# Two query tiles to a unit in a sparse attention, and conditioning by pairs of weight units

## The chip, the core and the metric

The kernel runs on one core of a Trainium2 chip: one program, one launch. The metric is the device time in microseconds (us), measured from outside the program; the profile's span is the time from the first to the last instruction on the core. The core has a matrix engine, TensorE (PE in the profile, PEld for its weight loads, PEq for its instruction queue), and VectorE (DVE), ScalarE (ACT), GpSimd (POOL) and SyncE (SP), which here issues most of the DMAs. The engines run side by side and wait for each other through semaphores. Each works through its own instructions in the order in which the program was written.

## What is computed

Four layers in a row on x (4 batches, 512 tokens, 512 channels), each steered by a vector of 512 numbers per batch. All numbers are float32.

```python
x = L0(x, cond)   # adaptive layer norm, sparse attention: 16 heads of 32, 4 key/value heads
x = L1(x, cond)   # adaptive RMS norm, attention: 8 heads of 64 on one key head; gated MLP of 2048
x = L2(x, cond)   # adaptive layer norm, attention: 16 heads of 32 with a bias; MLP of 2048
x = L3(x, cond)   # 8 experts of 64 channels, norm scaled and shifted by cond, output projection
```

The part that matters is layer 0:

```python
h = layernorm(x) * (1 + scale) + shift            # scale, shift: products of cond with W_ada
q = rope(h @ Wq.T); c = h @ Wkd.T
k, v = rope(c @ Wku.T), c @ Wvu.T                 # 4 heads, each used by 4 query heads
mask = (abs(i - j) > 64) & (j % 64 != 0) | (j // 128 > i // 128)    # hidden keys
y = softmax(q @ k.T / sqrt(32), hidden keys left out) @ v
x = x + y @ Wo.T
```

A tile of 128 queries therefore sees at most 197 keys: those of its own block of 128 and of the 64 before it (192 in all, or 128 for the first tile), and the earlier ones at multiples of 64 (1, 3 or 5).

The conditioning makes, from the vectors of the 4 batches, products with ten square weight matrices of 512 (tw1 and tw2 for layer 1; six for layer 2: two scales, two shifts, two gates; two for layer 3). In all but the first two, silu is taken of the vector first.

## The kernel before

**An order that is planned.** The kernel first runs as a plan. Every engine call and every matmul is recorded together with a start time that a small table of costs gives it (class Clocks); at the end all calls are sorted by these starts and emitted. So each engine's order is fixed when the program is built, and the chip's semaphores see to it that nothing starts too early.

**Streams.** Two streams of stages are woven together (interleave, streams A and M): layer 0 and layer 1's attention of a batch (a01), layer 1's MLP (m1), layer 2's attention (a2), layer 2's MLP with layer 3 (m2). A stage is a generator; it yields the amount of work just planned, or the time until which it must wait (Until), and the loop goes on with the stream that lags. At first batch 0 runs its a01 on stream M and batch 1 its own on stream A, both without an MLP beside them. From then on one stream has an attention while the other has an MLP. The conditioning is a third generator that moves when a stage asks for its result (wanted) or when no stream is ready.

**Units of attention.** The function attention takes units one by one: it issues the scores of unit i + 1, then turns the softened probabilities of unit i with TensorE's transposes (back), and, once two units have been turned, multiplies both with the values. The scores need all four PSUM banks of the pool psS (two_banks, a ring of 2); transposes and values use single banks (side.bank).

In layer 0 a unit is a pair (c, qt): four heads (one chunk c of 128 channels) and one tile of 128 queries, 16 units for each batch. Its steps are:

- scores: four matmuls with 32 rows each, in the four quarters of the array's rows, side by side; they write 128 to 197 columns into four banks.
- softmax: DVE adds the mask, scales and takes the lowest (lowest); ACT exponentiates and sums (soften); DVE takes the reciprocal of two sums; POOL multiplies. All of it runs in two halves of two heads.
- back: four transposes of the first 128 keys into a bank, and a copy into pT (evict, on ACT or DVE, whichever the plan has free); then four of the other 65 to 69 keys, if there are any, and another copy.
- values: for two units at once, matmuls with 32 columns each in the four quarters of the array's columns.

A run of matmuls on TensorE that follow each other in the same form of the array is called a run below. The forms here are the whole array (128*128 in the profile: projections, MLPs, transposes), row quarters (32*128: scores), column quarters (128*32: values and the conditioning's products with the vectors), and halves of both kinds (64*128 and 128*64).

**Conditioning.** For each of its ten weight units, partial makes four products with the vectors, one for each chunk of 128 rows, in the four column quarters; the result is evicted to rows. A second stage sums the four quarters: the matrix four has ones where a partition belongs to a batch, and four small matmuls (one per chunk) give the sums with channels on partitions. For the two gates one matmul of 512 columns gives them with batches on partitions, and they go to DRAM. The weight units pass one by one through a single buffer (ringC, tag late); the next is loaded when the products with the one before have been planned. Layer 1's norm asks for n1, its MLP for n2, layer 2 for all.

All engine calls of DVE, ACT, POOL and SP go through one wrapper and carry line 325 in the profile (load: line 391); matmuls have line 378, transposes line 384. So the profile's groups are told apart by their tiles: two are score banks, bank other PSUM banks, probs and wm the probabilities of the two streams, pT and hid the turned ones, arow the rows of the conditioning.

Of the kernel before, what the change touches and what calls it, by code (L numbers as in the profile page):

```python
# [19 lines left out]
P = 128  # L20
# [312 lines left out]
def cond_seq_kernel(ctx: ExitStack, tc: tile.TileContext, a: dict, out: bass.AP):  # L333
# [232 lines left out]
    cT, sT = (const.tile([P, NC, 32], F32, name=s) for s in ("cT", "sT"))  # L566
    gpsimd.memset(cT, 0.0)
    gpsimd.memset(sT, 0.0)
    four = const.tile([P, B], F32, name="four")
    vector.tensor_reduce(four, ident.rearrange("p (j b) -> p b j", b=32)[:, 0:B, :], axis=AX.X, op=ALU.add)  # L570
# [18 lines left out]
    vector.tensor_copy(cT[:, :, 0:B], condv)  # L589
    scalar.activation(sT[:, :, 0:B], condv, AF.Silu)  # L590
# [204 lines left out]
    def attention(side, units, scores, back, values, work, first, final=True):  # L795
# [21 lines left out]
        for i, u in enumerate(units):  # L817
            cost, more = 0.0, i + 1 < len(units)
            when = [scorable] if more else []
            if len(late) == 2:  # L820
                yield Until(*when, side.at, of=late[0][1] + late[1][1])
                values(late)
                late = []
                cost += 2 * work[1]
            else:
                yield Until(0.0, *when)
# [111 lines left out]
    def attention0(b, side):  # L938
# [71 lines left out]
        def scores(u):  # L1010
            c, qt = u
            first, near, seen = keys_of(qt)
            n = near + seen
            s = [two_banks() for _ in range(2)]
            for g in range(4):
                mm(
                    s[g // 2][:, g % 2, 0:n], lhsT=qT[quarter(g), c, qt * P : (qt + 1) * P],
                    rhs=kT[quarter(g), qt, 0:n], start=True, stop=True,
                )
            bias = mask[:, WIN - near : WIN + seen] if seen else mask[:, 64:WIN]  # L1020
            p = side.probs(WIN + 8)
            for q, sc in zip(p, s):
                soften(q, q, lowest(q, sc, bias, n, 1.0 / math.sqrt(32.0)), n, -1.0)
            return p, lambda: None
# [5 lines left out]
        def back(u, p, then):  # L1030
            if then:
                then()
            pT = part_of(side.pT(1)[0], 0, (2, 512))
            for i, (at, n) in enumerate(blocks(u[1])):
                yield Until(side.at, of=[q[:, :, at : at + n] for q in p])
                ps = side.bank()
                for g in range(4):
                    tr(ps[0:n, g * P : (g + 1) * P], p[g // 2][:, g % 2, at : at + n], ident)
                evict(pT[0:n, i, :], ps[0:n, :])
                yield 0.45  # L1040
            return [pT]

        def values(two):
            o, (c, first) = side.bank(), two[0][0]
            for k, ((_, qt), (pT,)) in enumerate(two):
                bl = blocks(qt)
                for i, (at, n) in enumerate(bl):
                    for g in range(4):
                        mm(
                            o[quarter(g), k * P : (k + 1) * P], lhsT=v[0:n, qt, i, quarter(g)],  # L1050
                            rhs=pT[0:n, i, g * P : (g + 1) * P], start=i == 0, stop=i == len(bl) - 1,
                        )
            evict(ctxT[:, c, first * P : (first + 2) * P], o[:, 0 : 2 * P])

        units = [(c, qt) for c in range(NC) for qt in range(NT)]
        yield from attention(side, units, scores, back, values, (0.7, 0.7), [qT, kT], False)
# [413 lines left out]
    def conditioning(side):  # L1470
        def partial(unit, cond):

            ps = side.bank()
            for i in range(NC):
                mm(
                    ps[32 * i : 32 * i + 32, :], lhsT=cond[:, i, :], rhs=unit[:, i, :], start=True, stop=True
                )
            rows = buf("arow", 2, (P, 512))
            evict(rows, ps)
# [4 lines left out]
        def product(name, cond):  # L1484

            unit = ringC.take(name)
            yield Until(side.at, of=[unit, sT])
# [306 lines left out]
```

## Time and profile before

| | us |
|---|---|
| three runs | 2446.61, 2450.02, 2448.89 |
| median | 2448.89 |
| the profiled execution | 2445.96 |
| its span | 2444.2 |
| TensorE's mean granted clock in it | 0.994 of full speed |

Groups of the profile that touch layer 0's units and the conditioning, all four batches (mean of one, number):

| group | mean ns | number |
|---|---|---|
| DVE: mask and lowest, 193 to 197 columns (probs) | 355 to 360 | 144 |
| DVE: mask and lowest, 128 columns (probs) | 287 | 48 |
| ACT: exponential, 193 to 197 columns (probs) | 446 to 450 | 144 |
| ACT: its sum read out (all exponentials on probs from SBUF) | 187 | 448 |
| DVE: reciprocal of two sums (all layers) | 165 | 320 |
| POOL: product with the reciprocal, 193 to 197 columns (probs) | 429 to 440 | 144 |
| ACT: copy of turned probabilities, 512 columns | 577 | 231 |
| DVE: the same | 683 | 172 |
| ACT: table load | 1283 | 32 |
| TensorE: bank<-four,arow, 4 columns (records) | 250 | 80 |

Durations of TensorE's records overlap, because matmuls are pipelined; what one costs is read from the starts of the ones that follow each other. A float32 matmul of the program leaves two records, a transpose one.

### The profile page before, as it was taken

Reading aid. Unit: us, or ns where it says so; the run is one execution under the profiler, and the core shown is the slowest. Engines: PE = TensorE matmul, PEld = TensorE weight load, DVE = VectorE, ACT = ScalarE, POOL = GpSimd, SP = SyncE. Lnnn points to the kernel's source line nnn. Section 1 sums busy time; section 2 is a strip of 40 time slices with the busy share of each in tenths; the row PEclk is TensorE's granted clock in tenths of the full one; section 3 lists DMA queues with packets and bytes.
Section 4 is the critical chain, followed back from the end, with each engine's and each line's share of the span. In section 5 each row is a group of like instructions: output and inputs, shape, how many; then the busy total and the mean of one; then the engine's idle time right before and its main releaser. Section 6 shows DMA issues by size and latency. Waiting matters only on the chain.

```text
span 2444.2 us, 33286 instructions
## 1 busy us (share of the span) xinstructions
PE 2408.0 (99%) x12586; PEld 1259.4 (52%) x12586; DVE 1118.8 (46%) x2886; ACT 870.0 (36%) x2088; POOL 725.8 (30%) x920
## 2 busy tenths in 40 slices
PE   8999999999999999999999999999999999999998
PEld 5555654444554555554455455564455544554444
DVE  5656452233654344535454445454455333673233
ACT  3745441002551351414454044241355202561213
POOL 5633320003332223323332222433322203442321
PEclk9999999999999999999999999999999999999999
DMA  3220212220112111121220212112211122112210
GB/s 112 70 74 34 72 69 70 90 87 35 35 53 92 54 67 56 36 73 46 80 70 29 97 53 74 52 40 73 73 48 53 61 80 88 36 36 88 89 52 26
DMA packets 80239, 154.17 MB, mean 63 GB/s; under 512 B 3584, under 2 KB 6688, under 8 KB 80080
## 3 DMA queue, kind: packets, MB, share of 16 engines
q1 hardware_dynamic: 79472, 151.83, 18.0%
q8 instruction: 100, 1.64, 0.3%
q14 instruction: 59, 0.48, 0.1%
q0 software_dynamic: 176, 0.15, 0.1%
q10 hardware_dynamic: 432, 0.07, 0.0%
HBM read 147.83 MB, written 4.21 MB: 62 GB/s over the span
## 4 chain that ended last, share of the span: by engine, by line
PE 95%; DVE 2%; ACT 1%; POOL 1%; DMA 1%; issue 1%; POOLq 0%; ACTq 0%; DVEq 0%
PE bank L378 72%; PE bank L384 12%; PE two L378 11%; ACT probs L325 1%; PE two L384 0%; DMA wm<-in_units 0%; DVE mn L325 0%; DVE mx L325 0%; ACT wm L325 0%; POOL inv L325 0%; DMA x<-in_x 0%; DVE nq L325 0%; POOL probs L325 0%; POOL rstd L325 0%; DMA arow<-in_rows 0%
## 5 line engine op out<-in xcount | busy, mean ns | idle before, releaser
L325 POOL TENSOR_SCALAR probs<-probs,inv 128x512 f32<-128x512 f32 (+4 forms) x544 | 316.3, 596 | 681.9 <-DVE inv L325 630.6
L325 ACT ACTIVATE probs<-probs,neg 128x512 f32<-128x512 f32 (+2 forms) x448 | 265.5, 594 | 215.6 <-DVE neg L325 209.6
L384 PEld LDWEIGHTS bank<-ident,probs 128*128 128x128 f32 (+2 forms) x1744 | 205.3, 141 | 162.8 <-issue 136.0
L378 PE MATMUL bank<-mT,wm_gate 128*128 128x512 f32 x512 | 246.9, 595 | 0.0
L384 PE MATMUL bank<-ident,probs 128*128 128x128 f32 (+2 forms) x1744 | 245.1, 275 | 0.8 <-POOL probs L325 0.4
L378 PE MATMUL bank<-mT,wm_up 128*128 128x512 f32 x512 | 245.5, 597 | 0.0
L378 PE MATMUL bank<-wm_down,hid 128*128 128x512 f32 x496 | 231.7, 596 | 0.0
L325 DVE CUSTOM_DVE_ANT_0 probs<-two,late 128x512 f32<-128x512 f32 x256 | 166.4, 688 | 79.2 <-PE two L378 48.1
L378 PE MATMUL bank<-wm_fc,hid 128*128 128x512 f32 x384 | 187.7, 593 | 0.0
L378 PE MATMUL bank<-mT,wm_fc 128*128 128x512 f32 x384 | 182.2, 596 | 0.0
L325 ACT COPY pT<-bank 128x512 f32<-128x512 f32 (+2 forms) x263 | 147.1, 577 | 82.7 <-PE bank L384 74.7
L325 ACT ACTIVATE mt<-bank 128x512 f32<-128x512 f32 x64 | 37.9, 591 | 322.2 <-PE bank L378 322.2
L378 PE MATMUL two<-kT,nq 32*128 32x512 f32 (+5 forms) x1088 | 149.8, 538 | 0.8 <-ACT probs L325 0.8
L325 DVE TENSOR_TENSOR x<-x,bank 128x512 f32<-128x512 f32 x98 | 66.9, 682 | 169.4 <-PE bank L378 169.4
L378 PEld LDWEIGHTS bank<-mT,wm_up 128*128 128x128 f32 x512 | 90.7, 190 | 97.8 <-issue 97.0
L378 PEld LDWEIGHTS bank<-mT,wm_gate 128*128 128x128 f32 x512 | 91.1, 190 | 94.7 <-issue 94.7
L378 PEld LDWEIGHTS bank<-wm_down,hid 128*128 128x128 f32 x496 | 89.2, 190 | 95.9 <-issue 94.2
L378 PEld LDWEIGHTS bank<-pT,v 128*32 128x32 f32 (+2 forms) x3488 | 112.7, 116 | 47.9 <-issue 28.1
L378 PE MATMUL bank<-pT,v 128*32 128x128 f32 (+2 forms) x3488 | 130.5, 274 | 0.0
L325 DVE COPY pT<-bank 128x512 f32<-128x512 f32 (+2 forms) x176 | 118.4, 683 | 22.3 <-PE bank L384 21.7
L325 POOL TENSOR_TENSOR rstd<-var,neg_half 128x4 f32<-128x4 f32 (+1 forms) x25 | 24.7, 991 | 347.5 <-DVE var L325 340.2
L378 PE MATMUL bank<-wa_q,h 128*128 128x512 f32 x272 | 127.7, 595 | 0.0
(283 smaller groups left out, 3363.7 us busy)
## 6 DMA issues: line engine op xcount, KB each, us to landing
wm_fc<-in_units SPq DMA_DIRECT2D x24, 1024.0 KB, 5.1
wm_gate<-in_units SPq DMA_DIRECT2D x16, 1024.0 KB, 5.1
wm_up<-in_units SPq DMA_DIRECT2D x16, 1024.0 KB, 5.5
wm_down<-in_units SPq DMA_DIRECT2D x16, 1024.0 KB, 5.4
wa_q<-in_units SPq DMA_DIRECT2D x10, 1024.0 KB, 5.0
wa_fc<-in_units SPq DMA_DIRECT2D x8, 1024.0 KB, 5.1
wa_o<-in_units SPq DMA_DIRECT2D x6, 1024.0 KB, 5.8
wa_k<-in_units SPq DMA_DIRECT2D x4, 1024.0 KB
```

Source lines behind the costliest of these rows:

```text
L325: return call(*map(real, args), **{k: real(x) for k, x in kw.items()})
L378: latest[0] = nc.tensor.matmul(real(out), lhsT=real(lhsT), rhs=real(rhs), **kw)
L384: latest[0] = nc.tensor.transpose(real(out), real(src), unit)
```

## The change

**Layer 0.** A unit becomes (c, (qt, qt + 1)): four heads and two query tiles, 8 units for each batch. Eight score matmuls fill both halves of each of the four banks, 256 columns apart. The softmax works on four parts at a time (two heads, two tiles) in each of its two halves; there is one reciprocal of four sums. The second half is planned in the midst of the transposes of the unit before, as in the other layers' attention. Transposes go by half and key block: both tiles' first blocks share a bank and one copy of 512 columns; the second blocks share a bank and are copied tile by tile (256 columns). Values follow each unit (group=1).

**Conditioning.** The vectors lie at columns 4 to 7 of 36 in cT and sT. A slice of 32 columns that begins at 4 puts them on rows 0 to 3 of each quarter, one that begins at 0 on rows 4 to 7. So two weight units' products are added (together) and one second stage with eight columns serves both. The ten units go in five pairs; the two gates are stored by one DMA.

```diff
-    cT, sT = (const.tile([P, NC, 32], F32, name=s) for s in ("cT", "sT"))
+    cT, sT = (const.tile([P, NC, 36], F32, name=s) for s in ("cT", "sT"))
-    four = const.tile([P, B], F32, name="four")
+    four = const.tile([P, 2 * B], F32, name="four")
...
-    def attention(side, units, scores, back, values, work, first, final=True):
+    def attention(side, units, scores, back, values, work, first, final=True, group=2):
...
-            if len(late) == 2:
-                yield Until(*when, side.at, of=late[0][1] + late[1][1])
+            if len(late) == group:
+                yield Until(*when, side.at, of=sum((pT for _, pT in late), []))
                 values(late)
                 late = []
-                cost += 2 * work[1]
+                cost += group * work[1]
...
         def scores(u):
-            c, qt = u
+            c, qts = u
             s = [two_banks() for _ in range(2)]
+            for k, qt in enumerate(qts):
+                first, near, seen = keys_of(qt)
+                for g in range(4):
+                    mm(
+                        s[g // 2][:, g % 2, 256 * k : 256 * k + near + seen],
+                        lhsT=qT[quarter(g), c, qt * P : (qt + 1) * P], rhs=kT[quarter(g), qt, 0 : near + seen],
+                        start=True, stop=True,
+                    )
+            p = side.probs(512)
+            def soft(i):
+                neg, total, inv = (tiny([P, 4], x) for x in ("neg", "total", "inv"))
...
+                for x, (q, sc, bias) in enumerate(parts):
+                    vector.tensor_tensor_reduce(
+                        out=q, in0=sc, in1=bias, scale=-1.0 / math.sqrt(32.0), scalar=HIGHEST,
+                        op0=ALU.add, op1=ALU.min, accum_out=neg[:, x : x + 1],
+                    )
+                for x, (q, _, _) in enumerate(parts):
+                    one = slice(x, x + 1)
+                    scalar.activation(q, q, AF.Exp, bias=neg[:, one], scale=-1.0, accum_out=total[:, one])
+                vector.reciprocal(inv, total)
+                for x, (q, _, _) in enumerate(parts):
+                    gpsimd.tensor_scalar(q, q, inv[:, x : x + 1], 1.0, ALU.mult, ALU.mult)
+            soft(0)
+            return p, lambda: soft(1)
...
         def back(u, p, then):
+            pTs = [part_of(t, 0, (2, 512)) for t in side.pT(2)]
+            for i in range(2):
+                for b in range(2):
+                    of = [(k, *blocks(qt)[b]) for k, qt in enumerate(u[1]) if b < len(blocks(qt))]
+                    yield Until(side.at, of=[p[i][:, :, 256 * k + at : 256 * k + at + n] for k, at, n in of])
+                    ps = side.bank().rearrange("p (j k q) -> p j k q", j=2, q=P)
+                    for k, at, n in of:
+                        for j in range(2):
+                            tr(ps[0:n, j, k, :], p[i][:, j, 256 * k + at : 256 * k + at + n], ident)
+                    dst = pTs[i][:, b, :].rearrange("p (j k q) -> p j k q", j=2, q=P)
+                    if b == 0:
+                        evict(pTs[i][:, b, :], ps.rearrange("p j k q -> p (j k q)"))
+                    else:
+                        for k, _, n in of:
+                            evict(dst[0:n, :, k, :], ps[0:n, :, k, :])
+                    if then and i == 0 and b == 1:
+                        then()
+                    yield 0.45
+            return pTs
...
-        units = [(c, qt) for c in range(NC) for qt in range(NT)]
-        yield from attention(side, units, scores, back, values, (0.7, 0.7), [qT, kT], False)
+        units = [(c, (qt, qt + 1)) for c in range(NC) for qt in range(0, NT, 2)]
+        yield from attention(side, units, scores, back, values, (1.4, 1.4), [qT, kT], False, group=1)
...
-        def partial(unit, cond):
+        def partial(unit, cond, u, rows):
...
-                    ps[32 * i : 32 * i + 32, :], lhsT=cond[:, i, :], rhs=unit[:, i, :], start=True, stop=True
+                    ps[32 * i : 32 * i + 32, :], lhsT=cond[:, i, 4 - 4 * u : 36 - 4 * u], rhs=unit[:, i, :],
+                    start=True, stop=True,
...
+            if u:
+                vector.tensor_tensor(rows, rows, ps, ALU.add)
+            else:
+                rows = buf("arow", 2, (P, 512))
+                evict(rows, ps)
...
+        def together(names, cond):
+            rows = None
+            for u, name in enumerate(names):
+                unit = ringC.take(name)
+                yield Until(side.at, of=[unit, cond] + ([rows] if u else []))
+                rows = partial(unit, cond, u, rows)
+                yield 1.1
             yield Until(side.at, of=[rows])
+            return rows
+        def product(names, cond):
+            rows, n = (yield from together(names, cond)), B * len(names)
             ps = side.bank()
             for c in range(NC):
-                mm(ps[:, c * B : (c + 1) * B], lhsT=rows[:, c * P : (c + 1) * P], rhs=four, start=True, stop=True)
+                mm(
+                    ps[:, c * n : (c + 1) * n], lhsT=rows[:, c * P : (c + 1) * P], rhs=four[:, 0:n],
+                    start=True, stop=True,
+                )
...
-        for label, unit, gain in (("n1", "tw1", V_LN1), ("n2", "tw2", V_LN2)):
-            v = yield from product(unit, cT)
+        vs = yield from product(("tw1", "tw2"), cT)
+        for label, v, gain in zip(("n1", "n2"), vs, (V_LN1, V_LN2)):
             vector.scalar_tensor_tensor(coef(label), v, 1.0, col(gain), ALU.add, ALU.mult)
...
+        s1, s2 = yield from product(("ada2_s1", "ada2_s2"), sT)
+        h1, h2 = yield from product(("ada2_t1", "ada2_t2"), sT)
+        rows = yield from together(("ada2_g1", "ada2_g2"), sT)
+        ps, row = side.bank(), buf("arow", 2, (P, 512))[0 : 2 * B, :]
+        mm(ps[0 : 2 * B, :], lhsT=four[:, 0 : 2 * B], rhs=rows, start=True, stop=True)
+        vector.tensor_tensor(row, ps[0 : 2 * B, :], t, ALU.add)
+        sync.dma_start(out=gates.rearrange("j b c -> (j b) c"), in_=row)
+        e1, e2 = yield from product(("emb_s", "emb_t"), sT)
```

## The prediction

> **What bounds the kernel now.** I read the page's busy shares and its chain first, then the busy time by stretches, then the timeline of TensorE.
>
> ```profile
> PE 2408.0 (99%) x12586; PEld 1259.4 (52%) x12586; DVE 1118.8 (46%) x2886; ACT 870.0 (36%) x2088; POOL 725.8 (30%) x920
> ...
> PE 95%; DVE 2%; ACT 1%; POOL 1%; DMA 1%; issue 1%; POOLq 0%; ACTq 0%; DVEq 0%
> ```
>
> TensorE is busy for 99% of the span and carries 95% of the chain that ended last. No other engine passes 46%. So a change counts only through TensorE's own work and through its waits.
>
> ```profile
> core 0: us, PE busy (x) PEld busy (x) DVE busy (x) ACT busy (x) POOL busy (x), PEclk, DMA share, GB/s
> ...
> 40.00:60.00 20.00, 16.22 (x90) 10.68 (x89) 10.82 (x42) 10.31 (x35) 15.61 (x22) 0.83 0.01 1
> 60.00:80.00 20.00, 19.97 (x163) 11.22 (x165) 11.81 (x54) 12.77 (x47) 17.63 (x31) 1.00 0.01 2
> ...
> 100.00:120.00 20.00, 18.74 (x192) 12.16 (x190) 13.83 (x82) 15.85 (x63) 9.54 (x24) 0.91 0.30 107
> 120.00:140.00 20.00, 17.70 (x206) 11.76 (x195) 12.60 (x62) 13.42 (x52) 9.59 (x24) 0.91 0.28 99
> ...
> 400.00:450.00 50.00, 50.00 (x118) 22.07 (x117) 14.30 (x27) 2.98 (x5) 1.02 (x1) 1.00 0.36 127
> ```
>
> The waits lie early. In the first 250 us, while layer 0 runs for batches 0 and 1 with no MLP beside it, TensorE idles here and there, and its granted clock falls to 0.83 and 0.91 in the stretches that hold such idling. From 400 us on it is full. In numbers: I compared the start-to-start step of each TensorE record with the step that its form takes elsewhere (429 ns for 512 columns, 109 for a transpose). What is over is 47.3 us before 400 us, 23.6 us from there to 2400, and 9.4 in the tail; 1.4 us before the first matmul and 3.9 after the last come on top. The other 2358.5 us are TensorE's steps themselves. The 15.4 us over between 60 and 200 us hold layer 0's units of the first two batches, 9.4 of them between 100 and 140.
>
> What the steps cost where nothing waits is seen in batch 2's layer-0 attention (columns: start, duration, engine, line, operation, tiles, array form, shape, records):
>
> ```profile
> 849.84 1.10 PE L384 MATMUL bank<-ident,probs 128*128 128x128 f32 x8
> 850.78 1.02 PE L378 MATMUL bank<-wm_down,hid 128*128 128x512 f32 x2
> 851.73 0.50 PE L378 MATMUL two<-kT,nq 32*128 32x128 f32 x8
> 852.16 1.98 PE L378 MATMUL bank<-wm_down,hid 128*128 128x512 f32 x4
> 853.99 1.04 PE L384 MATMUL bank<-ident,probs 128*128 128x128 f32 x8
> 854.86 1.88 PE L378 MATMUL bank<-wm_down,hid 128*128 128x512 f32 x4
> 856.67 1.09 PE L378 MATMUL bank<-pT,v 128*32 128x128 f32 x32
> 857.69 0.61 PE L378 MATMUL two<-kT,nq 32*128 32x193 f32 x8
> 858.23 0.66 PE L384 MATMUL bank<-ident,probs 128*128 128x128 f32 x4
> ```
>
> Read the starts, for the durations overlap. A program matmul is two records, a transpose one. From 850.78 to 851.73 are 0.95 us for two records of 0.429: so going from the whole array (128*128) to row quarters (32*128) costs 0.09. The four heads of a score run (four matmuls side by side, two passes) take 0.43 us at 128 columns and 0.54 at 193: 0.11 for 2 x 65 columns more, so 0.22 us is the streaming of 2 x 128 and 0.21 belongs to the run as such, its way back to the whole array included. A score run of its own costs 0.09 + 0.21 = 0.30 us (0.306 with the nanoseconds) beside its columns. One that directly follows a value run (856.67, then 857.69) shares that run's change.
>
> **The change, part by part.**
>
> *Score runs.* In layer 0, 16 units of one query tile per batch become 8 of two. Before, values came after each second unit, so 8 of the 16 score runs followed a value run and 8 stood alone. After, values follow each unit (group=1) and each score run but the first has one before it. The instruction order of the two programs agrees: 127 runs in row quarters before, 95 after, with the same number of score matmuls. 32 runs x 0.306 = 9.8 us off TensorE. The column counts stay, a second query tile in a run adds just its two passes.
>
> *Other runs.* Stand-alone runs gone should mean 64 fewer changes of array form; the order shows 520 runs before and 461 after, 59 fewer, because other work falls differently between them: 5 x 0.093 = 0.5 back, and a run of column quarters less, 0.05.
>
> *Conditioning.* Five of the ten second stages go: 16 of the matmuls with four (4 chunks x 4 pairs) and one of the two gate products.
>
> ```profile
> 118.50 0.95 PE L378 MATMUL bank<-four,arow 128*128 128x4 f32 x8
> 119.38 0.86 PE L378 MATMUL bank<-pT,v 128*32 128x128 f32 x24
> ```
>
> Eight records take 0.88 us, so 0.11 each (0.112): 16 x 2 x 0.112 = 3.6 us, and the gate product is 2 x 0.429 = 0.86. The remaining ones have 8 columns in place of 4; the records of bank<-wk,h with 128 columns also step by 0.112, so the width is free and the saving is that of whole instructions.
> The Trainium skill (TensorEngine Tiling (Array Packing), Instruction Overhead) speaks of some 60 cycles for a matmul however few its columns; at the 2.4 GHz of TensorE: Matmul & The Clock Gate (What's actually happening) that would be an estimate of 25 ns, and by it this item would be 0.8 us in place of 3.6. The row decides.
>
> *What is added elsewhere.* The second key block is evicted once per query tile: 48 copies of 512 columns become 96 of 256, which ACT does in 0.37 us against 0.58: +7.7 us over four batches on ACT and DVE. Five sums of rows on DVE (0.68) replace five evictions. Half as many reciprocals: 64 x 0.165 = 10.6 us less on DVE. ACT has 34 table loads for 32 (1.28 us each). All of it is hidden by TensorE's own work (ACT 36%, DVE 46%); with no cover the copies and the tables would show as 7.7 + 2.6 = 10.3 us. The stores of the gates are one DMA on SP's queue in place of two; the weight loads behind it wait once less.
>
> *A stage that moves.* The pair ends later. n1 now needs tw1 and tw2, with one load between them in the single buffer: its product stands in the order at 115 us of TensorE steps, where the norm of batch 0's layer 1 (four statistics of 0.69, a power of 1.0, four scalings of 0.5, some 6 us after the last output projection at 111) isn't done before 117 anyway. The last pair (emb) now closes at 484 us in place of 252, when layer 2 of batch 0 first asks for it; the load of the bias, 1 MB and about 5 us, is issued then. Behind this wait stand only layer 2's own transposes; TensorE meanwhile has the MLP of batch 1, and the first softmax that reads the bias is 69 us of steps later. Price nothing; without that MLP, four products, an eviction and the small DVE operations, about 3 us.
>
> *Waits.* A unit's first transposes now need four head parts softened, not two. In the rows:
>
> ```profile
> 59.63 0.44 ACT L325 ACTIVATE wm<-wm,neg 128x195 f32<-128x195 f32 x1
> ...
> 60.07 0.44 ACT L325 ACTIVATE wm<-wm,neg 128x195 f32<-128x195 f32 x1
> ...
> 60.74 1.68 POOL L325 TENSOR_SCALAR wm<-wm,inv 128x195 f32<-128x195 f32 x4
> ```
>
> Exponentials follow each other every 0.44 us, normalisations every 0.41. With a reduction (0.27) and a reciprocal (0.17) the chain to the first transposes was 0.27 + 2 x 0.44 + 0.17 + 2 x 0.41 = 2.1 us and is 0.27 + 4 x 0.44 + 0.17 + 4 x 0.41 = 3.8. Against it stands TensorE's work between a unit's scores and its first transposes, priced by the steps in each program's order: medians of 4.7 us (batch 0) and 5.05 (batch 1) before, 6.7 and 7.75 after. The margin grows from 2.6 and 2.9 to 2.9 and 3.9. In the new order batch 1's units also no longer alternate with the last of batch 0, which is where the 9.4 us of waits lie. Bounds: none of those 9.4 us goes, or all; on the loss side 1.7 us more of chain for each of the 16 units of these batches, 27.2. I take a third of the gain, 3.1 us, as the margin grows little.
>
> **Sum.** 9.8 - 0.5 + 0.05 + 3.6 + 0.86 = 13.8 us of steps and 3.1 of waits: 16.9. The profiled execution took 2445.96 us (span 2444.2), 2.9 below the median of 2448.89, which lies within the runs' own spread (2446.61 to 2450.02). From the median: 2432.0.
>
> **Rivals.**
> *The dense stretch empties.* All 9.4 us between 100 and 140 go, with both half-clock stretches. For it: the two attentions no longer overlap. Against it: conditioning and loads remain there. 2448.9 - 13.8 - 9.4 = 2425.7.
> *The early part gives its saving back.* POOL is 17.6 of 20 us busy between 60 and 80, with the angle tables between the normalisations; if it and ACT set the pace while there is no MLP, only batches 2 and 3 keep theirs, 16 x 0.306 = 4.9: 2444.0. Against it: TensorE is over its steps by only 2.0 us between 60 and 100.
> *The longer softmax is exposed* (the other side). In batches 0 and 1 TensorE stands before a unit's first transposes for the added 1.7 us, at worst 16 times: 2448.9 - 13.8 + 27.2 = 2462.3. It decides from where TensorE has less than 3.8 us between scores and transposes; in the order only the first unit (1.6 us) has, and there the second unit's scores had to wait for the reductions before too (2.3 us).
> *The merged run pays its 0.3 us for each query tile all the same.* Then only the 3.6 + 0.86 and the waits remain: 2441.3. Against it: in the rows 32 records in column quarters run at 0.11 a pass with no further cost.
>
> **How the numbers follow.** Forecast 0.62 (2427 to 2440, by the waits), dense stretch empties 0.13, saving given back 0.12, run cost kept 0.05, softmax exposed 0.08. 0.2% is 4.9 us, about what a measurement can tell: faster means below 2444.0, slower above 2453.8. Faster: 0.62 + 0.13 + 0.05 and a third of the one at 2444.0, 0.84. Same: the other two thirds, 0.08. Slower: 0.08. The range, 2423 to 2445, takes in the two rivals beside the forecast and leaves out the softmax one and the far end of the empty stretch.
>
> **What would show it.** In the profile after: 12552 matmul records; in batch 2's attention score runs of 16 records at about 0.43 + 0.33 us, with no 0.3 us between the tiles; 48 records of the products with four in place of 80; the granted clock between 100 and 140 us at 0.91 or better. The forecast is wrong if TensorE is busy for less than 99% in the first 300 us by more than now, above all ahead of transposes from wm and probs released by POOL.

## The result, and the profile after

| | before | after |
|---|---|---|
| median of six runs each (us) | 2446.70 (2444.41 to 2450.02) | 2431.39 (2429.84 to 2432.52) |
| span of the profiled execution (us) | 2444.2 | 2430.7 |
| TensorE's steps in it | 2358.5 | 2344.7 |
| over the steps (waits and half clock) | 80.2 | 80.5 |
| runs of one array form, of them in row quarters | 520, 127 | 461, 95 |

The ratio of the times is 0.9936 with a 95% interval of 0.9923 to 0.9948: 15.7 us less (12.7 to 18.8). "Steps" and "over" are worked out as in the prediction: each TensorE record's start to the next one's start, against what its form takes elsewhere. The steps fell by 13.8 us and the span by 13.5. The 13.8 come from the two instruction orders and the prices per form, so they confirm the order; whether the prices hold is seen from the times and from the rows of e5 and e6 below. "Over" is the rest of one execution. Executions of one kernel differ by some us, longer ones mostly at a lower clock: of sixteen of the kernel before, in the session of e1 to e4, the shortest took 2442.18 us at a granted clock of 0.996 and the longest 2451.20 at 0.992; and the profiled execution of the kernel after (2432.52) is the longest of its six. So the two values of "over", 80.2 and 80.5, don't settle by themselves whether it shrank.

The first lines are of the page of the kernel after, the busy shares and the chain that ended last (lines left out are marked by three dots).

```profile
PE 2392.8 (98%) x12552; PEld 1256.4 (52%) x12552; DVE 1116.7 (46%) x2854; ACT 868.6 (36%) x2105; POOL 725.9 (30%) x920
...
PE 95%; DVE 2%; ACT 1%; DMA 1%; POOL 1%; issue 0%; POOLq 0%; ACTq 0%; DVEq 0%
```

TensorE carries 95% of the chain as it did. It has 34 records fewer: 32 of the small products and 2 of the gate product. The score matmuls are all there; what went is the changes around them. Next, the timeline of TensorE in the kernel after, batch 2's layer-0 attention (columns as in the prediction).

```profile
840.68 0.86 PE L378 MATMUL bank<-pT,v 128*32 128x128 f32 x24
841.48 0.83 PE L378 MATMUL two<-kT,nq 32*128 32x128 f32 x16
842.24 1.09 PE L384 MATMUL bank<-ident,probs 128*128 128x128 f32 x8
...
847.58 1.09 PE L378 MATMUL bank<-pT,v 128*32 128x128 f32 x32
848.59 0.95 PE L378 MATMUL two<-kT,nq 32*128 32x195 f32 x16
849.47 1.13 PE L378 MATMUL bank<-wm_down,hid 128*128 128x512 f32 x2
```

Each score run now holds 16 records and follows a value run. From 841.48 to 842.24 is 0.76 us for a tile of 128 keys and one of 193, and from 848.59 to 849.47 is 0.88 for 195 and 197: two passes per tile and one way back to the whole array.

The third view is the busy time by stretches of the kernel after, with the granted clock behind the engines.

```profile
40.00:60.00 20.00, 16.27 (x95) 10.58 (x94) 9.88 (x38) 11.17 (x39) 14.21 (x18) 0.83 0.01 2
60.00:80.00 20.00, 18.84 (x202) 12.60 (x202) 16.62 (x75) 12.82 (x53) 17.68 (x35) 1.00 0.00 1
100.00:120.00 20.00, 17.25 (x152) 11.65 (x149) 8.48 (x32) 13.11 (x37) 5.25 (x11) 0.83 0.45 157
120.00:140.00 20.00, 20.00 (x158) 10.87 (x160) 14.44 (x69) 12.69 (x54) 9.10 (x24) 1.00 0.01 2
140.00:160.00 20.00, 17.37 (x164) 13.82 (x157) 13.96 (x58) 11.15 (x42) 8.29 (x18) 0.91 0.23 68
```

The waits moved. In the first 400 us TensorE's idle time, the stretch less its busy time, did not fall; the first line is the kernel before, the second the kernel after:

```profile
0.00:400.00 400.00, 377.96 (x2681) 229.90 (x2682) 212.71 (x686) 189.97 (x552) 157.97 (x270) 0.97 0.21 69
0.00:400.00 400.00, 376.22 (x2659) 228.81 (x2660) 215.41 (x669) 186.43 (x558) 158.23 (x270) 0.97 0.21 69
```

That is 22.0 us before and 23.8 after. Between 120 and 140 TensorE, which was busy for 17.70 us, is now busy for all 20; between 100 and 120 it fell from 18.74 to 17.25, and the clock there from 0.91 to 0.83. A mean of 0.83 over 20 us is 0.17 x 20 / 0.5 = 6.8 us at half clock. By the excess over the steps, in stretches of 20 us from 100 to 220: before 4.3, 5.1, 1.3, 1.3, 1.5, 4.6; after 6.8, 0.3, 5.7, 1.4, 3.7, 0.3. That is 18.1 us and 18.2 in these two executions; 2.7 of the 18.2 go when the same order runs without the half clock between 100 and 120 (e10, below).

Two places show what TensorE now waits for. The first is the chain in order of time of the kernel after, from 99 us on (start, duration, what).

```profile
99.48 0.59 POOL late L325
...
100.09 0.63 ACT late L325
...
100.74 1.28 ACT L325
...
102.04 1.25 ACT tab L325 x2
...
103.30 1.28 ACT L325
...
104.59 1.88 ACT wm L325 x8
```

This is ScalarE's queue: one of layer 1's angle tables (sines and cosines for its rotations), made by an absolute value and two sines (late, tab), with a load of the function table of 1.28 us before the sines and another after them. From 100.09 to 104.59 ACT works for the tables, and the exponentials of layer 1's attention (wm) stand behind. In the kernel before the same work ran from 85.39 to 89.87, and TensorE's timeline has no wait between 84 and 94 us. In TensorE's timeline of the same kernel the bracket tells the wait and its releaser:

```profile
102.93 0.85 PE L384 MATMUL bank<-ident,wm 128*128 128x128 f32 x6
104.89 1.39 PE L378 MATMUL bank<-wkv,pT 128*128 128x128 f32 x8 [1.11 <-DVE nq L325]
107.14 2.69 PE L378 MATMUL bank<-wkv,pT 128*128 128x128 f32 x10 [0.86 <-DVE t L325]
```

The second place is VectorE's queue, in TensorE's timeline and then in the chain.

```profile
143.69 1.39 PE L384 MATMUL bank<-ident,probs 128*65 128x128 f32 x8 [0.91 <-DVE arow L325]
146.14 1.06 PE L378 MATMUL bank<-four,arow 128*128 128x8 f32 x8 [1.07 <-DVE pT L325]
```

```profile
142.88 0.16 DVE var L325
143.04 0.61 DVE arow L325
143.69 0.45 PE bank L384 x2
```

Mask reductions (141.33 to 142.5), the next norm's statistics and then the new sum of rows (arow) stand in one queue. The sum reads the conditioning's product from a PSUM bank, and the stream has two single banks; so I read the 0.91 us as transposes that wait for a bank to come empty, and the 1.07 us likewise as the second stage that waits until VectorE, after four more mask reductions, has copied the turned probabilities (pT) out. A half-clock stretch of 3.4 us follows from 148.8 on.

### The profile page after: what moved, and what is told of

Its sections match the earlier page's. It is cut to its first block, busy times and chain, and to the rows that moved or that the text cites. A ratio compares the mean times of both kernels' runs of the same rounds, so it can differ in the third digit from the quotient of the medians.

```text
span 2430.7 us, 32979 instructions
## 1 busy us (share of the span) xinstructions
PE 2392.8 (98%) x12552; PEld 1256.4 (52%) x12552; DVE 1116.7 (46%) x2854; ACT 868.6 (36%) x2105; POOL 725.9 (30%) x920
## 3 DMA queue, kind: packets, MB, share of 16 engines
q1 hardware_dynamic: 79472, 151.83, 18.2%
## 4 chain that ended last, share of the span: by engine, by line
PE 95%; DVE 2%; ACT 1%; DMA 1%; POOL 1%; issue 0%; POOLq 0%; ACTq 0%; DVEq 0%
PE bank L378 72%; PE bank L384 12%; PE two L378 11%; ACT probs L325 0%; PE two L384 0%; DMA wm<-in_units 0%; DVE mx L325 0%; ACT wm L325 0%; POOL inv L325 0%; DMA x<-in_x 0%; DVE nq L325 0%; DVE mn L325 0%; DVE probs L325 0%; DMA arow<-in_rows 0%; DVE t L325 0%
## 5 line engine op out<-in xcount | busy, mean ns | idle before, releaser
L384 PEld LDWEIGHTS bank<-ident,probs 128*128 128x128 f32 (+1 forms) x1744 | 206.6, 141 | 173.8 <-issue 141.3
L384 PE MATMUL bank<-ident,probs 128*128 128x128 f32 (+1 forms) x1744 | 246.7, 275 | 3.9 <-ACT pT L325 1.5
L378 PE MATMUL two<-kT,nq 32*128 32x512 f32 (+5 forms) x1088 | 142.4, 529 | 0.4 <-ACT probs L325 0.4
L325 DVE COPY pT<-bank 128x512 f32<-128x512 f32 (+3 forms) x199 | 124.8, 640 | 13.7 <-PE bank L384 12.8
```

The costliest lines, as they stand in the source:

```text
L325: return call(*map(real, args), **{k: real(x) for k, x in kw.items()})
L378: latest[0] = nc.tensor.matmul(real(out), lhsT=real(lhsT), rhs=real(rhs), **kw)
L384: latest[0] = nc.tensor.transpose(real(out), real(src), unit)
```

## Experiments

All times in us; the ratio is to the kernel before on the same chip, with its 95% interval. "Over" is the excess over TensorE's steps, where it was worked out.

| run | median (range) | ratio | span | over |
|---|---|---|---|---|
| e1 layer 0 alone | 2438.44 (2435.54 to 2441.76) | 0.9971 (0.9960 to 0.9983) | 2436.8 | 82.2 |
| e2 conditioning alone | 2445.92 (2444.98 to 2449.15) | 1.0001 (0.9992 to 1.0010) | 2445.5 | 86.6 |
| e3 values of two units | 2430.82 (2427.26 to 2433.69) | 0.9935 (0.9921 to 0.9949) | 2431.9 | 84.1 |
| e4 no sine tables | 2427.59 (2426.20 to 2429.98) | 0.9927 (0.9915 to 0.9940) | 2424.4 | 74.2 |
| e5 extra beside | 2437.26 (2435.82 to 2438.43) | 0.9962 (0.9950 to 0.9974) | 2435.5 | |
| e6 extra between | 2452.47 (2448.54 to 2455.58) | 1.0023 (1.0014 to 1.0032) | 2448.7 | |
| e7 second stages twice, in before | 2455.69 (2453.03 to 2460.44) | 1.0040 (1.0027 to 1.0053) | 2452.2 | |
| e8 the same, in after | 2435.61 (2432.84 to 2437.78) | 0.9956 (0.9944 to 0.9968) | 2433.7 | |
| e9 after, waits filled | 2428.70 (2426.08 to 2432.32) | 0.9931 (0.9918 to 0.9943) | 2425.1 | 66.8 |
| e10 e3 in batches 2 and 3 | 2430.85 (2426.62 to 2435.17) | 0.9940 (0.9926 to 0.9953) | 2428.5 | 79.6 |
| e11 before, waits filled | 2443.69 (2441.26 to 2447.10) | 0.9992 (0.9983 to 1.0001) | 2441.9 | 69.8 |
| e12 e9 and e10 together | 2426.18 (2425.81 to 2426.95) | 0.9920 (0.9908 to 0.9933) | 2424.5 | 67.5 |

### The two parts, each alone (e1, e2)

e1 takes layer 0's part into the kernel before, e2 the conditioning's.

```diff
# e1, against before
-        units = [(c, qt) for c in range(NC) for qt in range(NT)]
-        yield from attention(side, units, scores, back, values, (0.7, 0.7), [qT, kT], False)
+        units = [(c, (qt, qt + 1)) for c in range(NC) for qt in range(0, NT, 2)]
+        yield from attention(side, units, scores, back, values, (1.4, 1.4), [qT, kT], False, group=1)
...
# e2, against before
-        for label, unit, gain in (("n1", "tw1", V_LN1), ("n2", "tw2", V_LN2)):
-            v = yield from product(unit, cT)
+        vs = yield from product(("tw1", "tw2"), cT)
+        for label, v, gain in zip(("n1", "n2"), vs, (V_LN1, V_LN2)):
...
```

> Only layer 0's units of two tiles; the conditioning is that of before. Theory (the time is TensorE's steps plus waits that stay as they were): by the order of its instructions TensorE's steps are 2349.2 us against 2358.5 before (462 runs against 520), so 9.3 us less: 2437.4 from a median of 2446.7. Rival (the saving came from the conditioning and from waits around it): less than 5 us less. In the profile the sum of what TensorE is over its steps should stay near 80 us.

> Only the conditioning by pairs; layer 0 is that of before. Theory: steps 2353.4 us, so 5.1 less: 2441.6 from 2446.7. Rival (half of the conditioning's waits in the first 300 us go as well, as each second stage was waited for on the path): 8 us less or more. Together with the run of layer 0 alone the two should give 14.4, against 13.8 of steps for both.

By steps, which follow from the instruction orders, the parts add: -9.3 us in e1 and -5.1 in e2 make -14.4, against -13.8 for both. By the time they do not. e1 gained 7.1 us (4.2 to 9.8) and e2 nothing (between 2.0 less and 2.4 more), 6.9 in all, where both together gained 15.7. In the profiled executions the excess shows where it went: +2.0 in e1 and +6.3 in e2 (86.6 against 80.2), but only +0.3 with both. TensorE's idle time in the first 400 us says the same: 28.2 us in e1 and 26.6 in e2, against 22.0 before and 23.8 with both. Conditioning by pairs gave its whole saving back in the plan of the old layer 0; its forecast of 2441.6 and the rival's 8 us or more both missed. One place of that is plain in TensorE's timeline. In e2:

```profile
107.70 0.50 PE L378 MATMUL two<-kT,nq 32*128 32x128 f32 x8
108.98 0.93 PE L378 MATMUL two<-kT,nq 32*128 32x193 f32 x8 [0.78 <-ACT hid L325]
```

And in the kernel before:

```profile
106.38 0.50 PE L378 MATMUL two<-kT,nq 32*128 32x128 f32 x8
107.11 1.06 PE L378 MATMUL bank<-four,arow 128*128 128x4 f32 x8 [0.23 <-ACT arow L325]
108.10 0.61 PE L378 MATMUL two<-kT,nq 32*128 32x193 f32 x8
```

The second stage that the pair saves stood between two score runs and covered the wait of the second; without it TensorE idles for 0.78 us there, and the half-clock stretch behind it is 6.8 us in place of 3.4 (over the first 400 us, though, both executions have 20.5 us at half clock). Elsewhere in e2 the excess is 1.2 us up in the first 20 us, 1.7 up between 240 and 260, and 1.2 down between 120 and 140. The first is no more than the 1.4 us by which the kernel after and e10, whose orders are the same there, differ in their first 20 us. Why the others moved was not tried.

### Values of two units in one run (e3, e10)

```diff
-            o, (c, qts), pTs = side.bank(), *late[0]
+            o, (c, first) = side.bank(), late[0][0]
+            for (_, qts), pTs in late:
...
-        yield from attention(side, units, scores, back, values, (1.4, 1.4), [qT, kT], False, group=1)
+        yield from attention(side, units, scores, back, values, (1.4, 1.4), [qT, kT], False)
```

e10 has group=1 if b < 2 else 2 in that call.

> The changed kernel, but with values after each second unit of two tiles, so four tiles in one run and one copy of 512 columns. Theory: 443 runs against 461, steps 2342.3 against 2344.7, so 2.4 us less than the changed kernel, 2429.0 from 2431.4 and 16.2 less than before. Rival: the values come in lumps, the score banks stay shut for longer and TensorE waits more in the first 200 us: no gain or up to 5 us more.

> The changed kernel with values by two units only for batches 2 and 3, where the MLP of another batch stands beside them; batches 0 and 1 keep values by unit. 451 runs against 461, steps 2343.4 against 2344.7. Theory (with values by two units everywhere the gain of 2.4 us was given back in the first 120 us alone): the first 300 us are as in the changed kernel, the waits after 400 us too, so 1.3 us less, 2430.1 from 2431.4. Rival: waits after 700 us grow by more than 1 us.

e3's steps are 2.4 us fewer (2342.3), but its excess is 3.6 more in the profiled execution, the longest of its five; most of it lies in the first 100 us, 27.2 against 19.9, where its half-clock stretch from 58 us on is 10.2 us long. Its time cannot be told from the change's. e10 keeps the early part as it was: steps -1.3, span -2.2, and again no difference that the times show; 1.3 of the 2.2 lie before 840 us, where its order of TensorE's records is that of the change.

### What a score run costs (e5, e6)

One small matmul of 32 columns on the whole array is added to each layer-0 unit: in e5 ahead of its first transposes, where the array is in that form anyway, in e6 between the score matmuls of its two tiles.

```diff
+    def with_extra(call, out):
+        def emit():
+            latest[0] = nc.tensor.matmul(real(out), lhsT=real(ident), rhs=real(ident[:, 0:32]), start=True, stop=True)
+
+        start, n, after = clocks.program[-1]
...
# e5, in back
+                            if i == 0 and b == 0 and k == 0 and j == 0:
+                                with_extra("before", ps[:, 0, 0, 0:32])
# e6, in scores
+                if k == 0:
+                    with_extra("after", s[1][:, 1, 208:240])
```

> The changed kernel with one small extra matmul (128 rows and columns of the identity, 32 columns out) for each of layer 0's 32 units, put in front of the unit's first transpose, where TensorE works with the whole array; every order stays. It is the control of the next run. Steps 7.1 us more (32 x 2 x 0.112). Expected by both theories: 2438.5 from 2431.4, somewhat less where TensorE waits just before it in the first 200 us.

> The same 32 extra matmuls, but each stands between the score matmuls of the unit's two tiles, so that TensorE leaves the row quarters and comes back; every other order stays. Theory (a score run of its own costs 0.306 us beside its columns): steps 9.8 us more than in the control, 16.9 more than in the changed kernel, 2448.3, about the time of the kernel before. Rival (a run costs little, the gain came from the softmax and its waits): within 3 us of the control.

e6 takes 15.2 us more than e5 in the medians and 13.2 in the spans, for 9.8 forecast: 0.48 or 0.41 for each of 32 units, waits included. With its extras it is slower than the kernel before (1.0023). TensorE's timeline of e6 shows one, with 195 and 197 keys:

```profile
858.69 0.61 PE L378 MATMUL two<-kT,nq 32*128 32x195 f32 x8
859.23 0.41 PE L390 MATMUL two<-ident 128*128 128x32 f32 x2
859.57 0.62 PE L378 MATMUL two<-kT,nq 32*128 32x197 f32 x8
860.12 1.12 PE L378 MATMUL bank<-wm_down,hid 128*128 128x512 f32 x2
```

And of e5:

```profile
844.31 0.41 PE L390 MATMUL bank<-ident 128*128 128x32 f32 x2
844.55 1.07 PE L384 MATMUL bank<-ident,probs 128*128 128x128 f32 x8
...
852.72 0.30 PE L390 MATMUL bank<-ident 128*128 128x32 f32 x2
852.86 0.63 PE L384 MATMUL bank<-ident,probs 128*128 128x128 f32 x4
```

From 858.69 to 860.12 are 1.43 us, against 0.88 for the merged run of the kernel after: 0.55 for the split. The extra's own step in e5 is 0.24 us when it follows scores (844.31 to 844.55) and 0.14 when it follows whole-array work (852.72 to 852.86). What it adds is read over its neighbours too, record by record against the kernel after: 0.22 and 0.17. So leaving row quarters and coming back costs 0.33 to 0.38 us; the forecast had 0.306.

The same cost can be read without the extra and without any price. Between the two lines below lies batch 3's layer-0 attention, in the kernel before and then in the kernel after:

```profile
1173.74 1.88 PE L378 MATMUL bank<-mT,wm_gate 128*128 128x512 f32 x4
...
1764.28 1.88 PE L378 MATMUL bank<-mT,wm_gate 128*128 128x512 f32 x4
```

```profile
1163.13 1.88 PE L378 MATMUL bank<-mT,wm_gate 128*128 128x512 f32 x4
...
1750.81 1.88 PE L378 MATMUL bank<-mT,wm_gate 128*128 128x512 f32 x4
```

The stretch takes 590.54 us before and 587.68 after, with the same number of matmul records, 2.6 us of waits and a clock of 1.00 in both, and 24 score runs for 32: 2.86 us for 8 runs, 0.36 each. From e5 to e6, where 8 runs are put back, it grows from 589.24 to 592.10 us, 2.86 again.

### Whether the small products are on the path (e7, e8)

```diff
+    def twice():
+        start, n, once = clocks.program[-1]
+        clocks.program[-1] = (start, n, lambda: (once(), once()))
...
                 mm(ps[:, c * B : (c + 1) * B], lhsT=rows[:, c * P : (c + 1) * P], rhs=four, start=True, stop=True)
+                twice()
```

The edit is e7's; e8's is the same call behind the matmul with eight columns. The second stages for layers 1 to 3 are issued twice: 32 matmuls more in the kernel before (e7), 16 more in the kernel after (e8).

> The kernel before with each of the 32 small matmuls with four in the second stages of the conditioning issued twice (the same result); every order stays. Steps 7.2 us more. Theory A (these matmuls lie on the path; the conditioning alone gained nothing because its new plan happened to wait more elsewhere): 7 us more than before, 2452.4 from 2445.2. Theory B (they fill time in which TensorE would wait anyway, so removing them turns into waits): 3 us more or less.

> The changed kernel with its 16 small matmuls with four issued twice, every order as it is. Steps 3.6 us more. Theory A: 3.6 us more, 2435.0 from 2431.4. Theory B: 1.5 us more or less.

64 records more made the span 8.0 us longer in e7 (7.2 of steps, 9.2 in the medians), and 32 made it 3.0 longer in e8 (3.6 of steps, 4.2 in the medians of two sessions). TensorE's timeline of e8 and of the kernel after has the last of these stages:

```profile
535.69 1.85 PE L378 MATMUL bank<-four,arow 128*128 128x8 f32 x16
537.39 3.68 PE L378 MATMUL bank<-mT,wm_gate 128*128 128x512 f32 x8
```

```profile
534.45 0.95 PE L378 MATMUL bank<-four,arow 128*128 128x8 f32 x8
535.26 3.68 PE L378 MATMUL bank<-mT,wm_gate 128*128 128x512 f32 x8
```

1.70 us for 16 records and 0.81 for 8: the 8 more take 0.111 each, with 8 columns as with 4.

The Trainium skill (TensorEngine Tiling (Array Packing), Instruction Overhead) has some 60 cycles of overhead for each matmul. The prediction's estimate of 25 ns, worked out from that figure, would have made it 1.6 us in e7 and 0.8 in e8; the runs do not agree with it.

### What the waits are worth (e4, e9, e11, e12)

In e4 ScalarE copies in place of the absolute value and the two sines of layer 1's tables, so that no table load is needed there.

```diff
+        def copied(dst, src):
+            if engine is gpsimd:
+                start, n, _ = clocks.program[-1]
+                clocks.program[-1] = (start, n, lambda: nc.scalar.copy(real(dst), real(src)))
+
         scalar.activation(e, r, AF.Abs)
+        copied(e, r)
...
```

> The changed kernel with the two sines and the absolute value of layer 1's angle tables replaced by copies of the same size on ACT, so that layer 1 gets other angles; every order stays as it is. This takes 2.6 us of table loads (sine and back to exponentials) off ACT at 100 to 104.6 us, in the middle of a unit's softmax. Theory (the waits of 6.8 us that the changed kernel has between 100 and 120 come from ACT being held there, with a stretch at half clock behind it): those waits fall by 3 to 6 us and the time with them, 2425 to 2428. Rival (they come from the passage from batch 0's units to batch 1's, keys and values first): less than 1 us.

The view by stretches and TensorE's timeline of e4, at the same place:

```profile
100.00:120.00 20.00, 17.74 (x159) 11.10 (x156) 9.53 (x39) 10.15 (x37) 5.16 (x10) 1.00 0.46 158
```

```profile
104.11 1.38 PE L378 MATMUL bank<-wkv,pT 128*128 128x128 f32 x8 [1.11 <-DVE nq L325]
105.86 1.92 PE L378 MATMUL bank<-wkv,pT 128*128 128x128 f32 x10 [0.36 <-DVE t L325]
```

The wait of 1.11 us stays, so it was not the tables'; the one of 0.86 becomes 0.36. The clock is 1.00 where it was 0.83: the 6.8 us at half clock are gone, and the excess between 100 and 120 falls from 6.8 to 3.7. That the half microsecond did this is not shown. e10 keeps the angle tables; up to 840 us its instructions on TensorE, VectorE, ScalarE and GpSimd are those of the kernel after, in the same order. It has at this place:

```profile
100.00:120.00 20.00, 17.22 (x184) 11.36 (x184) 8.48 (x32) 13.67 (x38) 6.64 (x14) 1.00 0.46 157
```

```profile
106.26 1.38 PE L378 MATMUL bank<-wkv,pT 128*128 128x128 f32 x8 [1.12 <-DVE nq L325]
108.51 1.92 PE L378 MATMUL bank<-wkv,pT 128*128 128x128 f32 x10 [0.87 <-DVE t L325]
```

The same waits, the clock at 1.00, and the part from 106 to 116 us done 2.7 us sooner. So 0.5 us of what e4 gains here is the tables'; the rest is also there without the edit, in one execution and not in another. Over the whole kernel e4's span is 6.3 us shorter, but that is the shortest of its five executions against the longest of the change's six. The medians say 3.8 and the ratios 2.2, with intervals that overlap those of the change. Whether the shorter wait makes a half-clock stretch rarer stays open.

The kernels have a function that fills TensorE's planned waits in the first 30 us with matmuls whose results nobody reads. e9 lets it go on to 300 us in the kernel after, e11 in the kernel before.

```diff
-        if count > 1 and until < 30.0:
+        if count > 1 and until < 300.0:
```

> The changed kernel, with the rule that fills planned waits of TensorE with idle products of the identity (keep_up, before only up to 30 us of the plan) extended to 300 us: 37 small matmuls, 8.1 us of steps, in the places where the plan sees TensorE wait. Theory (a wait of some microseconds costs its own length and then as much again in a stretch at half clock): the fillers stand in time that is lost anyway, the half-clock stretches at 53, 108 and 149 us go, and 3 to 7 us are saved: 2424 to 2428. Rival (the plan's waits aren't those of the chip): the fillers add to the path, 2433 to 2439, and half-clock stretches stay.

> The kernel before with the same extended filling as the changed kernel had in the run with filled waits: 36 small matmuls more, steps 2366.7 against 2352.8 there. Theory (the change takes TensorE steps off, whatever becomes of the waits): it stays 13 to 15 us above the changed kernel with filled waits, 2443 from its 2428.7, so 2 to 4 us faster than the kernel before. Rival (the change's gain was partly one of waits): less than 9 us apart.

37 matmuls more in e9 add 8.1 us of steps, and the excess falls by 13.7 (80.5 to 66.8); in e11 36 add 8.2, and it falls by 10.4. Three of e9's stretches:

```profile
40.00:60.00 20.00, 17.06 (x121) 11.51 (x120) 12.10 (x51) 11.79 (x42) 15.66 (x23) 1.00 0.01 2
100.00:120.00 20.00, 18.38 (x166) 10.94 (x165) 10.77 (x54) 13.92 (x55) 7.59 (x17) 1.00 0.35 125
140.00:160.00 20.00, 18.97 (x176) 13.25 (x176) 10.85 (x45) 9.22 (x34) 8.39 (x19) 1.00 0.02 5
```

The clock is 1.00 in all three (0.83, 0.83 and 0.91 in the change), though TensorE still stands for 1 to 3 us in each. With the filling the first 400 us hold 3.4 us at half clock in e9, e11 and e12 alike, for 23.9 in the change and 20.5 before. The net is small: 5.6 us of span in e9 and 2.3 in e11, and in the times neither can be told from its own kernel without the filling; e9's median lies just above its forecast of 2424 to 2428. What the pair tells is the worth of the change where the mean granted clock is 0.998 in both (0.994 and 0.993 without the filling): 15.0 us by the medians and 16.8 by the spans, for 13.9 of steps.

e12 is e9 with e10's call:

> The changed kernel with both edits, filled waits and values by two units in batches 2 and 3. Steps 2351.5 against 2352.8 with filled waits alone: 1.3 us less, 2427.4 from 2428.7, if both edits keep their worth; the rival is that the new order waits more in the first 300 us, no change or up to 3 us more.

Its five runs lie between 2425.81 and 2426.95, all below the change's lowest of 2429.84, though the intervals of the two ratios overlap. It is the fastest of all, some 20 us under the kernel before.

## Why the prediction was right, and where it was not

*The total.* 2431.39 against 2432.0. Part of the closeness is luck: the forecast started from the median of three runs, 2448.89, and that of six is 2446.70. The drop is 15.3 us between the medians and 13.5 in the spans, for 16.9 forecast. Part is two errors that offset each other: the score runs were worth more than their price, and the waits did not fall (both below). The range, 2423 to 2445, also held three of the four rivals (2425.7, 2441.3 and 2444.0), so it is the experiments and not the total that tell them apart.

*Score runs, right, and priced somewhat low.* 127 runs became 95, with 0.76 us for a run of a 128-column and a 193-column tile, as 0.43 + 0.33 said. Batch 3's stretch shows 0.36 a run, and so does e6 against e5 from the other side; at that price 32 runs are 11.4 us, not 9.8, if batches 0 and 1 save what 3 does. The rival that each tile pays its 0.3 us anyway falls with that.

*Other runs, right.* 59 fewer in all, in the trace as in the instruction order; the steps of that order come to 13.8 us less, which is the sum of this and the two items beside it.

*Conditioning, right in steps.* 48 records of the products with four; e7 and e8 show that each costs 0.111 on the path. But that it is worth 4.5 us by itself does not hold: e2 gained nothing, with more waits in its profiled execution. The forecast's sum speaks of both parts together, and there it came out.

*The stage that moves, right.* No wait on coef or the bias shows between 400 and 700 us; the excess there is 1.7 us against 1.9 before. Nor do the added copies show: ACT and DVE are busy for 1.4 and 2.1 us less than before, all in all.

*Waits: the step that failed.* "I take a third of the gain, 3.1 us, as the margin grows little." TensorE's idle time in the first 400 us was 22.0 us before and 23.8 after, and 24.6 in e10, whose order is the same up to 840: about 2 us more, not 3.1 less. The prediction's own sign of being wrong, TensorE less busy in the first 300 us than before, came, by 1.4 us. By place, the 9.4 us of excess between 100 and 140 became 7.1 (2.7 less in e10), and 4.4 more came between 140 and 160. The forecast priced each wait at the place where the kernel before had it. A new plan puts the same ACT and DVE work beside other TensorE work: the angle tables, in a stretch without waits before, now hold up layer 1's exponentials, which costs 0.5 us (e4); and, as I read it, PSUM banks come empty late where the new sum of rows shares VectorE's queue with the mask reductions. A better entry would have been zero with some 6 us to both sides: the idle time of the first 400 us rose by 6.1 us in e1, 4.6 in e2 and 3.4 in e3.

*The clock: not a sign that one execution can give.* "The granted clock between 100 and 140 at 0.91 or better" held from 120 to 140 (1.00), not from 100 to 120 (0.83); in e10 the same order has 1.00 in both.

*The other rivals.* The longer softmax would have cost up to 27 us ahead of transposes released by POOL; one such wait came, of 1.2 us, for one of 0.4 before. The others that came are ACT's and DVE's queues, and the excess of the first 140 us is 27.0 against 28.6. The early part did not give the score runs' saving back when both parts were made, and the dense stretch emptied only in its second half.

*Still open.* Why the conditioning alone takes its saving back in waits is shown at one place only, and why both parts together wait less than either alone not at all. What the waits of a plan come to was not foreseen by any step here.

## What to carry to other kernels

Where one engine is full, price a change by the starts of its records and count the changes of array form: here 0.36 us out of row quarters and back, and 0.11 for a record of few columns, come to some 15 us, about what was gained. Waits of a planned kernel are not a sum that a part of it carries along: two parts that save 9.3 and 5.1 us of steps gained 7.1, nothing, and 15.7 together, so test the parts together as well as alone. Put zero for the waits, a range on both sides, and do not read a stretch of low clock in one profile as the work of the edit before the same order has run twice. Then look at what other work the new order places ahead of the critical queue.

## What the runs showed of the hardware

A wait can cost twice. The half-clock stretches of the first 400 us come in lengths of 3.4, 6.8 and 10.2 us behind waits that are themselves much shorter: ahead of the one from 108 us on TensorE's longest single wait is 1.11 us. In each execution they begin whole multiples of 3.41 us apart, but not at the same places of the program: in the kernel after at 12.26, 53.22, 107.83, 148.79 and 237.54 us, in e10, with the same order there, at 54.67, 146.83 and 235.58. So the same waits cost a stretch in one execution and none in another (2.7 us between these two, from 106 to 116).

The Trainium skill (TensorE: Matmul & The Clock Gate, What's actually happening) has windows of about 3.4 us, with the clock halved after one that was idle. The lengths agree with such windows. That a whole window must stand idle does not: between 100 and 120 us TensorE was busy for 17.25 of 20 us, and no wait there was half as long as a window; in the 3.41 us ahead of 107.83 it was busy for 61%. How much of a window must be idle no run here shows.

A small matmul's cost depends on its neighbours: the same 32-column one added 0.17 us behind whole-array work and 0.22 behind scores.
